# Rows 0 and 3 of the last image: separate even and odd products, other points added by VectorE, and a new order of the last two and a half images

## The chip, the core and the metric

The kernel runs on one core of a Trainium2 chip. The metric is device time in microseconds (us) of one execution; a profile of one execution gives the times of single instructions, counted from the start of its span.

## What is computed

Sixteen images of 128 channels by 64 x 64 pixels go through two layers, each with a group normalization in front and a residual sum behind it. Layer 0 is a 3 x 3 convolution of quantized inputs, done three times with three sets of weights; each of the three results is rounded to integers and clipped before they are summed. Layer 1 is an attention-like step made of 1 x 1 convolutions.

```python
def layer0(x):                      # x: 16 x 128 x 64 x 64
    v = round(clip(gn(x), -1, 1) * 127) / 127 * 0.6
    fv = patches(v) + 0.1 * patches(v) ** 3            # 3 x 3, padded by 1
    outs = [einsum(fv, g_pos[i] - g_neg[i]) for i in range(3)]
    mem = adc(outs[2])                                  # adc: scale, round, clip
    for i, bit in enumerate((2, 1, 0)):
        mem = mem + adc(outs[i]) * 2 ** bit
    return mem * output_factor + bias

def layer1(x):                      # as 64 x 128 by 128 x 4096 products
    q, k, v = Wq @ gn(x), Wk @ gn(x), Wv @ gn(x)
    num, den = exp(B) @ (exp(k) * v), exp(B) @ exp(k)
    return Wm @ (q * num / den)

y = x + layer0(x);  out = y + layer1(y)
```

## The kernel before, in words

**Convolution by points.** The 3 x 3 convolution is done with fewer products than nine. The rows of an image are cut into 16 tiles of four output rows. Each tile is turned into six sums of input rows, "points" 0 to 5 (`point`, L497). Each point is convolved along the columns, and the four output rows are sums of the points. Output rows 1 and 2 of every tile are handled together (half `h = 0`), rows 0 and 3 together (`h = 1`). Points 1 to 4 need sums that two output rows share; point 0 or point 5 belongs to one half only.

**A block** (`Block`, L562) is one image with one of the three weight sets `i`. It has two halves in PSUM, and each is a list of small operations whose names appear in the order lists, with the number `k = 2 i + h` of the half behind a dot. For one half of points 1 to 4, `u` is 0 or 1: `q1u q2u q0u q3u` are four TensorE products into `pa` and `pb` (L556); `m1u` (L579), `sdu` (L581) and `sAu` (L584) are ScalarE copies out of `pa` between them; `Bo` (L587) and `df` (L588) are VectorE sums, and `sm` is the last sum, by VectorE for an odd `k` (L594) and by an accumulating DMA from GpSimd's queue for an even `k` (L596).

The rest of a block (`rest`, L645) does the output rows. `ma` and `mc` (`middle`, L610) write two rows of small integers from the point sums. `S0` and `S3` (`total`, L615 and L618) are the sums of the other points. Then follow, for even and odd output columns in one two-bank PSUM tile: `P` (`shared`, L621), one product into one of the two banks; `bc` (`spread`, L625), VectorE, which puts that product plus the other points' sums in both banks; `o0 o1` (`outer`, L630), four products accumulated on top; `tk` (`take`, L633), ScalarE, which writes both banks as int16 into the integer tile; `bA` or `bB` (`bound`, L636), VectorE's clip; `aA` or `aB` (`add`, L641 or L643), the sum over weight sets, by VectorE or by a DMA. So the products `o0 o1` wait for `bc`, and `bc` waits for the point sums.

**The last block of the last image** (`Last`, L665) has the same work under other names: `tma tmc` are `middle`, `tS0 tS1` `total`, `tP0 tP1` `shared`, `tbc tbd` `spread`, `to0 to1` and `tp0 tp1` `outer` for rows 1 and 2 and for rows 0 and 3, `tk0 tk3` `take`, `tb0` to `tb3` `bound`, `ta0` to `ta3` the sum into `acc` by VectorE (L684). Rows 1 and 2 use the PSUM tile `py`, rows 0 and 3 use `pb`. The `h` of the code is 0 for rows 1 and 2 and 1 for rows 0 and 3.

**The end of an image** (`End`, L687): `cx0` to `cx3` scale the summed integers to float (ScalarE, L699), `cd0x` to `cd3x` add the input by accumulating DMAs (GpSimd's queue, L702), `sq0` to `sq3` square and sum (ScalarE, L364) as soon as a chunk's DMA has landed, and `ya pmy yb pvy yc yl yd` turn the sums into the normalization: VectorE and ScalarE on single columns, and two tiny products (`pmy` L383, `pvy` L392). For the last image the input is loaded early into the space of `gmat` (`Lx0` to `Lx3`, SyncE's queue, L717), added by VectorE row by row (`tx`, L724), and squared by ScalarE (`ts`); its normalization is `tna` to `tnd`.

**Layer 1** runs in four chunks ("pairs") of an image: `xn` normalizes (ScalarE, L796); `kp vp qp dn op` are products; `ek g ln ex` are ScalarE's, `ekv u oa ob oc` VectorE's; `r` (ScalarE, L782) adds the bias, `rd` (GpSimd's queue, L812) adds the input by a DMA, `st` (SyncE's queue, L813) stores. Chunks 0 and 2, and 1 and 3, share one buffer, so `xn2` waits for the store `st0` and `xn3` for `st1`. The last image has its own buffers and names with a capital (`Xn Kp Vp ...`).

**Order.** Every engine executes its instructions in the order in which the program issues them, and the program issues them by lists written out in the source. `ORDER` serves most images; `LAST` (L155) serves the end, from the middle of the last image but one. An entry such as `m10.3+1` is operation `m10.3` of turn 16 - 1 = 15, the last image's (turns count from 0); `+2` is the image before it, `+0` the tail behind it. In turn 15 the halves `.0` and `.1` of the rest, the `cx cd sq y` operations and the pairs belong to images before the last.

Of the kernel before, what the change touches and what calls it, by code (L numbers as in the profile page):

```python
# [94 lines left out]
START = "x0 xa pmx xb pvx xc xl xd gr0 er0 cp gr1 er1 pb1 pa1 cs1 cq1 cd1"  # L95

LAST = """
    cl0+2 sA1.2+2 S3.2+2 q31.2+2 lj3+2 st2+2 q10.3+2 cl1+2 P.2+2 bc.2+2 m10.3+2 q11.3+2 m11.3+2
    s0+2 q20.3+2 q21.3+2 o0.2+2 Bo.2+2 va0+2 s1+2 va1+2 sd0.3+2 o1.2+2 bA.2+2 sd1.3+2 q01.3+2
    sq1+2 sq2+2 lj2+2 gr0+2 sq3+2 q30.3+2 q00.3+2 tk.2+2 sA1.3+2 er0+2 q31.3+2 sA0.3+2 ya+2  # L100
    df.2+2 n3+2 n2+2 pmy+2 yb+2 P.3+2 bc.3+2 Bo.3+2 cp+2 q11.4+2 pvy+2 q10.4+2 yc+2 cl3+2
    df.3+2 o0.3+2 m10.4+2 m11.4+2 o1.3+2 q20.4+2 q21.4+2 yl+2 s3+2 yd+2 xn0+2 sd0.4+2 sd1.4+2
    kp0+2 vp0+2 sm.3+2 tk.3+2 P.4+2 q01.4+2 cl2+2 sm.2+2 ek0+2 va3+2 mc.4+2 s2+2 st3+2 aA.2+2
    S0.4+2 ekv0+2 bc.4+2 dn0+2 sA1.4+2 g0+2 q00.4+2 sA0.4+2 va2+2 u0+2 xn1+2 ln0+2 o1.4+2 gr1+2
    o0.4+2 q30.4+2 oa0+2 ex0+2 kp1+2 er1+2 tk.4+2 qp0+2 ob0+2 vp1+2 q11.5+2 ma.4+2 oc0+2 S3.4+2
    ek1+2 m11.5+2 pb0+2 op0+2 r0+2 ekv1+2 q31.4+2 Bo.4+2 rd0+2 q10.5+2 pa0+2 m10.5+2 st0+2
    P.5+2 q20.5+2 df.4+2 bc.5+2 sd0.5+2 q21.5+2 sd1.5+2 dn1+2 q00.5+2 g1+2 bB.3+2 xn2+1 bA.4+2
    q01.5+2 q30.5+2 o1.5+2 o0.5+2 u1+2 cs0+2 oa1+2 ln1+2 cd0+2 q31.5+2 ex1+2 tk.5+2 sA1.5+2
    sA0.5+2 cq0+2 aB.3+2 sm.4+2 kp2+1 qp1+2 vp2+1 ob1+2 ek2+1 aA.4+2 Bo.5+2 oc1+2 q10.0+1 op1+2
    m10.0+1 q20.0+1 r1+2 q11.0+1 m11.0+1 P.0+1 sd0.0+1 df.5+2 sm.5+2 ekv2+1 mc.0+1 S0.0+1  # L110
    q21.0+1 dn2+1 bB.5+2 q00.0+1 bc.0+1 o1.0+1 o0.0+1 rd1+2 g2+1 u2+1 sA0.0+1 ln2+1 aB.5+2
    sd1.0+1 ma.0+1 st1+2 q30.0+1 oa2+1 ex2+1 ob2+1 tk.0+1 xn3+1 pb1+2 S3.0+1 q01.0+1 bA.0+1
    qp2+1 oc2+1 pa1+2 kp3+1 op2+1 r2+1 vp3+1 ek3+1 cs1+2 cq1+2 ekv3+1 q31.0+1 P.1+1 bc.1+1
    q10.1+1 m10.1+1 sA1.0+1 Bo.0+1 df.0+1 rd2+1 dn3+1 o0.1+1 g3+1 u3+1 oa3+1 ln3+1 ex3+1 o1.1+1
    tk.1+1 q11.1+1 q20.1+1 cd1+2 aA.0+1 qp3+1 m11.1+1 bB.1+1 q21.1+1 sd0.1+1 q00.1+1 ob3+1
    sm.0+1 oc3+1 op3+1 sd1.1+1 aB.1+1 sA0.1+1 r3+1 q30.1+1 cx1+1 p0+1 e0+1 rd3+1 q01.1+1 cx0+1
    sA1.1+1 q31.1+1 Bo.1+1 q10.2+1 m10.2+1 df.1+1 q11.2+1 q20.2+1 cd1x+1 p5+1 y0+1 cd0x+1 P.2+1
    cx2+1 cd2x+1 m11.2+1 sd0.2+1 q21.2+1 q00.2+1 cx3+1 sd1.2+1 q01.2+1 q30.2+1 sA0.2+1 sq0+1
    sm.1+1 q10.3+1 mc.2+1 S0.2+1 q31.2+1 cd3x+1 bc.2+1 e5+1 o0.2+1 ma.2+1 sq1+1 o1.2+1 S3.2+1
    sA1.2+1 Lx0+0 m10.3+1 tk.2+1 Bo.2+1 bA.2+1 q11.3+1 m11.3+1 q20.3+1 P.3+1 df.2+1 q21.3+1  # L120
    sd0.3+1 q00.3+1 bc.3+1 Lx1+0 o1.3+1 sq2+1 sd1.3+1 q30.3+1 st3+1 sq3+1 sA0.3+1 st2+1 ya+1
    pmy+1 yb+1 q31.3+1 pvy+1 yc+1 yl+1 Bo.3+1 q01.3+1 sA1.3+1 yd+1 sm.2+1 df.3+1 sm.3+1 q10.4+1
    m10.4+1 mc.4+1 o0.3+1 xn0+1 S0.4+1 q11.4+1 tk.3+1 kp0+1 vp0+1 P.4+1 ek0+1 ekv0+1 q20.4+1
    bc.4+1 xn1+1 dn0+1 g0+1 u0+1 sd0.4+1 o0.4+1 m11.4+1 oa0+1 ln0+1 o1.4+1 ex0+1 q21.4+1 ob0+1
    tk.4+1 kp1+1 ma.4+1 qp0+1 vp1+1 aA.2+1 oc0+1 S3.4+1 ek1+1 op0+1 ekv1+1 sd1.4+1 r0+1 q00.4+1
    q01.4+1 sA1.4+1 P.5+1 rd0+1 dn1+1 g1+1 bc.5+1 q11.5+1 bA.4+1 o1.5+1 st0+1 o0.5+1 sA0.4+1
    q30.4+1 u1+1 q10.5+1 aA.4+1 ln1+1 tk.5+1 oa1+1 ex1+1 xn2+0 qp1+1 ob1+1 q31.4+1 oc1+1 bB.3+1
    Bo.4+1 op1+1 kp2+0 r1+1 m10.5+1 vp2+0 aB.3+1 q20.5+1 df.4+1 ek2+0 m11.5+1 ekv2+0 sd0.5+1
    q21.5+1 sd1.5+1 dn2+0 q30.5+1 q01.5+1 g2+0 u2+0 ln2+0 oa2+0 rd1+1 q31.5+1 sA1.5+1 st1+1
    q00.5+1 qp2+0 bB.5+1 ex2+0 aB.5+1 Bo.5+1 xn3+0 sA0.5+1 kp3+0 vp3+0 ob2+0 oc2+0 op2+0 ek3+0  # L130
    r2+0 df.5+1 tma+0 ekv3+0 sm.5+1 tS1+0 dn3+0 g3+0 u3+0 ln3+0 tP1+0 tbd+0 ex3+0 qp3+0 sm.4+1
    oa3+0 ob3+0 oc3+0 tp0+0 op3+0 tmc+0 tS0+0 tb2+0 tp1+0 Lx2+0 Lx3+0 r3+0 tP0+0 tb1+0 ta1+0
    tbc+0 to1+0 tx1+0 ta2+0 tk3+0 tx2+0 tb3+0 tsh+0 to0+0 ta3+0 tk0+0 tb0+0 ts1+0 ta0+0 ts2+0
    tx0+0 ts0+0 tx3+0 ts3+0 tna+0 tpm+0 rd2+0 tnb+0 tpv+0 tnc+0 tnl+0 tnd+0 Xn0+0 Xn2+0 Xn1+0
    Kp0+0 rd3+0 Ek0+0 Vp0+0 Xn3+0 Kp1+0 Eq0+0 Dn0+0 Vp1+0 Gg0+0 Uu0+0 Ek1+0 Eq1+0 Oa0+0 Ln0+0
    Ex0+0 Qp0+0 Kp2+0 Dn1+0 Gg1+0 Ob0+0 Oc0+0 Vp2+0 st3+0 Uu1+0 st2+0 Ek2+0 Eq2+0 Oa1+0 Ln1+0
    Ex1+0 Op0+0 Ob1+0 Qp1+0 Oc1+0 Dn2+0 Rr0+0 Op1+0 Kp3+0 Rd0+0 Gg2+0 Vp3+0 Qp2+0 Uu2+0 Rr1+0
    Rd1+0 St0+0 St1+0 Ek3+0 Oa2+0 Ln2+0 Eq3+0 Ex2+0 Dn3+0 Gg3+0 Ob2+0 Oc2+0 Uu3+0 Op2+0 Oa3+0
    Ln3+0 Ex3+0 Xa2+0 Qp3+0 Ob3+0 Xb2+0 Sa2+0 Sb2+0 Oc3+0 Op3+0 Xa3+0 Sa3+0 Xb3+0 Sb3+0
# [4 lines left out]
def conv_preact_kernel(  # L144
# [410 lines left out]
    def mm(o, w, r, start, stop):  # L555
        pe.matmul(  # L556
            o if len(r.shape) == 2 else o.rearrange("p (t w) -> p t w", w=W2), w, r,
            start=start, stop=stop, skip_group_check=True,
        )
# [398 lines left out]
```

## Time and profile before

| | |
|---|---|
| median of 3 runs | 1602.0 us (1598.37 to 1602.01) |
| profiled execution, device time | 1598.49 us |
| its span in the profile | 1596.8 us |
| TensorE busy, whole span | 1487.7 us (93%) |
| VectorE / ScalarE / GpSimd busy | 1479.8 / 1183.0 / 224.0 us |
| granted TensorE clock, mean | 0.981 |

The profile page lists busy time by engine. The trace behind it can be asked for stretches of time, for single instructions in order of time (start, duration, engine, line, operation, output and inputs, and in brackets how long the engine sat idle before and what ended that), for the DMAs issued in a stretch with their time to landing, and for the chain of work that ended last. A product of 128 x 128 weights with 512 columns shows as two TensorE records, which together take 0.86 us when products follow each other.

### The profile page before, as it was taken

Reading aid. Unit: us, or ns where it says so; the run is one execution under the profiler, and the core shown is the slowest. Engines: PE = TensorE matmul, PEld = TensorE weight load, DVE = VectorE, ACT = ScalarE, POOL = GpSimd, SP = SyncE. Lnnn points to the kernel's source line nnn. Section 1 sums busy time; section 2 is a strip of 40 time slices with the busy share of each in tenths; the row PEclk is TensorE's granted clock in tenths of the full one; section 3 lists DMA queues with packets and bytes.
Section 4 is the critical chain, followed back from the end, with each engine's and each line's share of the span. In section 5 each row is a group of like instructions: output and inputs, shape, how many; then the busy total and the mean of one; then the engine's idle time right before and its main releaser. Section 6 shows DMA issues by size and latency. Waiting matters only on the chain.

```text
span 1596.8 us, 14936 instructions
## 1 busy us (share of the span) xinstructions
PE 1487.7 (93%) x4680; PEld 563.4 (35%) x4680; DVE 1479.8 (93%) x1919; ACT 1183.0 (74%) x1857; POOL 224.0 (14%) x250
## 2 busy tenths in 40 slices
...
GB/s 186 79 92 120 103 160 171 126 204 114 148 128 164 184 119 196 120 137 141 150 205 109 156 131 150 166 132 203 117 152 132 156 176 121 196 66 119 119 158 80
DMA packets 67361, 227.03 MB, mean 142 GB/s; under 512 B 7632, under 2 KB 8272, under 8 KB 67280
## 3 DMA queue, kind: packets, MB, share of 16 engines
q0 software_dynamic: 37904, 123.42, 42.1%
...
## 4 chain that ended last, share of the span: by engine, by line
PE 58%; DMA 14%; issue 11%; DVE 11%; ACT 5%; POOL 2%; DVEq 0%; POOLq 0%; ACTq 0%; SPq 0%
PE py L556 19%; PE pa L556 18%; DMA x<-in_x_dram 5%; PE pz L749 5%; PE pb L556 5%; PE pz L759 3%; PE py L749 3%; DMA s<-s 3%; DMA acc<-y 3%; PE py L771 3%; ACT x L699 2%; DVE acc L610 1%; ACT gs L364 1%; DVE y L610 1%; DVE s L615 1%
## 5 line engine op out<-in xcount | busy, mean ns | idle before, releaser
L556 PE MATMUL py<-v,ud 128*128 128x512 f32 x760 | 357.0, 608 | 1.9 <-DVE py L625 1.3
L556 PE MATMUL pa<-cs,us 128*128 128x512 f32 x384 | 199.1, 620 | 41.7 <-DVE cs L514 31.9
L556 PE MATMUL pa<-cd,us 128*128 128x512 f32 x384 | 203.9, 622 | 11.7 <-ACT pb L581 11.7
L556 PE MATMUL pa<-cq,us 128*128 128x512 f32 x384 | 198.1, 612 | 11.3 <-ACT d L579 11.2
L556 PEld LDWEIGHTS py<-v,ud 128*128 128x128 f32 x760 | 138.9, 189 | 184.0 <-issue 148.9
L556 PE MATMUL pb<-cd,us 128*128 128x512 f32 x384 | 194.5, 602 | 1.9 <-ACT pb L581 1.7
L579 ACT ACTIVATE d<-pa 128x512 f32<-128x512 f32 x192 | 112.2, 594 | 37.8 <-PE pa L556 28.0
L812 POOL DMA_DIRECT2D xn<-x x60 | 59.9, 998 | 567.8 <-ACT xn L782 567.5
L581 ACT ACTIVATE pb<-pa 128x512 f32<-128x512 f32 x192 | 112.5, 586 | 31.3 <-PE pa L556 30.7
L584 ACT ACTIVATE s<-pa 128x512 f32<-128x512 f32 x192 | 110.4, 591 | 32.0 <-PE pa L556 29.9
L749 PE MATMUL pz<-xn,w 128*64 128x512 f32 x480 | 121.8, 607 | 1.3 <-ACT xn L796 1.2
L587 DVE SCALAR_TENSOR_TENSOR s<-d,pb 128x1024 f32<-128x1024 f32 x96 | 117.2, 1221 | 3.6 <-PE pb L556 3.2
L643 POOL DMA_DIRECT2D acc<-y x62 | 68.5, 1105 | 360.8 <-DVE y L636 212.2
L588 DVE TENSOR_TENSOR d<-s 128x1024 f32<-128x1024 f32 x96 | 117.5, 1224 | 1.6 <-ACT s L584 1.5
L633 ACT ACTIVATE y<-py 128x1024 int16<-128x1024 f32 x63 | 84.0, 1334 | 46.0 <-PE py L556 44.8
L782 ACT ACTIVATE xn<-py,scalars 128x512 f32<-128x512 f32 x120 | 76.0, 685 | 56.1 <-PE py L771 56.0
L556 PEld LDWEIGHTS pa<-cs,us 128*128 128x128 f32 x384 | 66.3, 191 | 139.6 <-issue 67.0
L556 PEld LDWEIGHTS pa<-cq,us 128*128 128x128 f32 x384 | 68.0, 190 | 119.5 <-issue 69.4
L556 PEld LDWEIGHTS pa<-cd,us 128*128 128x128 f32 x384 | 66.4, 190 | 123.6 <-ACT pb L581 56.9
L556 PEld LDWEIGHTS pb<-cd,us 128*128 128x128 f32 x384 | 70.2, 190 | 96.0 <-issue 85.2
L556 PE MATMUL py<-sv,ud 128*128 128x512 f32 x190 | 97.7, 596 | 3.3 <-ACT y L633 3.2
L596 POOL DMA_DIRECT2D s<-s x48 | 45.9, 956 | 339.5 <-DVE d L588 127.9
...
## 6 DMA issues: line engine op xcount, KB each, us to landing
xc<-in_x_dram SPq DMA_DIRECT2D x121, 512.0 KB, 5.6
acc<-y POOLq DMA_DIRECT2D x62, 512.0 KB, 5.5
x<-in_x_dram POOLq DMA_DIRECT2D x60, 512.0 KB, 10.4
xn<-x POOLq DMA_DIRECT2D x60, 512.0 KB, 4.9
out_dram<-xn SPq DMA_DIRECT2D x60, 512.0 KB, 5.1
s<-s POOLq DMA_DIRECT2D x48, 512.0 KB, 6.3
gmat<-in_x_dram SPq DMA_DIRECT2D x5, 512.0 KB, 8.9
x<-in_g_neg_dram SPq DMA_DIRECT2D x2, 576.0 KB, 11.4
```

Source lines behind the costliest of these rows:

```text
L556: pe.matmul(o if len(r.shape) == 2 else o.rearrange("p (t w) -> p t w", w=W2), w, r, start=start, stop=stop, skip_group_check=True,)
L579: f"m1{u}.{k}": lambda u=u, a=a: act.activation(d[:, u], a, AF.Copy),
L581: f"sd{u}.{k}": lambda a=a, b=b: act.activation(b, a, AF.Copy, scale=-1.0),
L584: f"sA{u}.{k}": lambda u=u, a=a: act.activation(s[:, u, 0], a, AF.Copy),
L587: f"Bo.{k}": lambda: dve.scalar_tensor_tensor(s[:, :, 1], d, 2.0, pb, ALU.mult, ALU.add),
L588: f"df.{k}": lambda: dve.tensor_tensor(d, s[:, 1], s[:, 0], ALU.subtract),
L633: act.activation(self.column(self.part(1)[0], h), y, AF.Copy)
L643: pool.dma_start(a, y, accum_op=ALU.add)
L749: pe.matmul(self.tiles(o)[h * IC : (h + 1) * IC], w, x[:, t[0] : t[1] : t[2]], start=True, stop=True)
L759: pe.matmul(o[c, t], eb[r, c], self.half(x)[r, t], start=True, stop=True, skip_group_check=True)
L782: act.activation(g[:, t], self.tiles(self.op[h]), AF.Identity, bias=bias_sb)
L812: "rd": lambda: pool.dma_start(self.r, self.x2, accum_op=ALU.add),
```

## The change

In the last block of the last image, for both halves: `shared` now makes its product once for each of the two banks, so even and odd columns start with a product of their own, and `outer` accumulates on it with nothing in between. `spread` (`tbc`, `tbd`) is gone. `take` by ScalarE is replaced by `complete`, a VectorE instruction that adds the products in PSUM and the other points' sums and writes int16. Rows 0 and 3 use the PSUM tile `pz` in place of `pb`.

The list `LAST` is written anew as a whole: 570 entries in place of 572, the same operations otherwise, in another order on all queues. Other blocks and lists are untouched.

```diff
-        def shared(self, h, y):
-            mm(y[:, 1], ud[self.i][:, h, 0], sv[:, h], True, True)
+        def shared(self, h, y, c=1):
+            mm(y[:, c], ud[self.i][:, h, 0], sv[:, h], True, True)
...
     class Last(Block):
+        def complete(self, h, y):
+            t = self.d[0] if h else ss[1][:, 1]
+            dve.tensor_tensor(self.column(self.part(1)[0], h), y, t, ALU.add)
...
-            for h, z in ((0, py), (1, pb)):
+            for h, z in ((0, py), (1, pz)):
                 o |= {
-                    f"tS{h}": lambda h=h: self.total(h), f"tP{h}": lambda h=h, z=z: self.shared(h, z),
-                    f"tb{'cd'[h]}": lambda h=h, z=z: self.spread(h, z), f"tk{3 * h}": lambda h=h, z=z: self.take(h, z),
+                    f"tS{h}": lambda h=h: self.total(h),
+                    f"tP{h}": lambda h=h, z=z: [self.shared(h, z, c) for c in range(2)],
+                    f"tk{3 * h}": lambda h=h, z=z: self.complete(h, z),
                 }
```

The parts of the order that matter below, taken from the two lists and sorted by queue (entries of other queues left out):

```diff
 ScalarE, last image but one, its second layer
-g1+2 xn2+1 ln1+2 ex1+2 tk.5+2 sA1.5+2 sA0.5+2 ek2+1
+g1+2 sd0.5+2 sd1.5+2 ln1+2 tk.5+2 xn2+1 ex1+2 sA0.5+2 sA1.5+2 ek2+1
 VectorE, the same stretch, earlier
-yd+2 sm.3+2 cl2+2 va3+2 mc.4+2 S0.4+2 ekv0+2 bc.4+2
+yd+2 ma.4+2 sm.3+2 S3.4+2 mc.4+2 va2+2 cl3+2 S0.4+2 ekv0+2 bc.4+2
 ScalarE, last image
-r3+1 cx1+1 cx0+1 sA1.1+1 m10.2+1 cx2+1 m11.2+1 sd0.2+1 cx3+1 sd1.2+1 sA0.2+1
+sA1.1+1 r3+1 sA0.1+1 cx0+1 m10.2+1 cx2+1 cx1+1 sd0.2+1 m11.2+1 cx3+1 sA0.2+1 sd1.2+1
 ScalarE, directly after
-sq0+1 sq1+1 sA1.2+1 m10.3+1 tk.2+1 m11.3+1 sd0.3+1 sq2+1 sd1.3+1 sq3+1
+sA1.2+1 sq0+1 sq1+1 sq2+1 m10.3+1 m11.3+1 tk.2+1 sd0.3+1 sd1.3+1 sq3+1
 TensorE, the same stretch
-o0.2+1 o1.2+1 q11.3+1 q20.3+1 P.3+1 q21.3+1 q00.3+1 o1.3+1 q30.3+1 pmy+1 q31.3+1
+q11.3+1 o0.2+1 o1.2+1 q20.3+1 q21.3+1 P.3+1 q00.3+1 q01.3+1 q30.3+1 pmy+1 q31.3+1
 SyncE's queue
-st1+2 Lx0+0 Lx1+0 st3+1 st2+1 st0+1 st1+1 Lx2+0 Lx3+0
+st1+2 st3+1 st2+1 Lx0+0 Lx1+0 Lx2+0 Lx3+0 st0+1 st1+1
 ScalarE, end of the last image
-ex2+0 xn3+0 sA0.5+1 ek3+0
+ex2+0 xn3+0 sA0.5+1 sA1.5+1 ek3+0
 TensorE, end of the last image
-q01.5+1 q31.5+1 q00.5+1 qp2+0 kp3+0 vp3+0 op2+0 dn3+0 tP1+0 qp3+0 tp0+0 op3+0 tp1+0 tP0+0 to1+0 to0+0
+q00.5+1 q01.5+1 q31.5+1 qp2+0 kp3+0 vp3+0 op2+0 dn3+0 qp3+0 tP1+0 tp0+0 op3+0 tp1+0 tP0+0 to1+0 to0+0
 VectorE, end of the last image
-df.5+1 tma+0 ekv3+0 sm.5+1 tS1+0 u3+0 tbd+0 oa3+0 ob3+0 oc3+0 tmc+0 tS0+0 tb2+0 tb1+0 ta1+0 tbc+0 tx1+0 ta2+0 tx2+0 tb3+0 tsh+0 ta3+0 tb0+0 ta0+0 tx0+0 tx3+0
+df.5+1 sm.5+1 ekv3+0 tma+0 tb1+0 u3+0 oa3+0 ta1+0 ob3+0 tS1+0 oc3+0 tmc+0 tb2+0 tx1+0 tsh+0 tS0+0 tk3+0 ta2+0 tb3+0 ta3+0 tx2+0 tk0+0 tb0+0 ta0+0 tx0+0 tx3+0
 ScalarE, second layer of the last image
-Xn1+0 Ek0+0 Xn3+0 Gg0+0 Ek1+0 Ln0+0 Ex0+0 Gg1+0 Ek2+0 Ln1+0 Ex1+0 Rr0+0 Gg2+0 Rr1+0
+Xn1+0 Ek0+0 Gg0+0 Ek1+0 Ln0+0 Ex0+0 Gg1+0 Ek2+0 Ln1+0 Ex1+0 Rr0+0 Xn3+0 Gg2+0 Rr1+0
```

More of the change, by code (lines that the diff above doesn't have):

```diff
@@ L97 @@
 LAST = """
[L98 to L139, printed above, removed]
+    q31.2+2 S3.2+2 cl1+2 lj3+2 sA1.2+2 P.2+2 q10.3+2 m10.3+2 lj2+2 q11.3+2 q20.3+2 bc.2+2 s1+2
@@ new lines @@
+    cl0+2 m11.3+2 Bo.2+2 o1.2+2 s0+2 sd0.3+2 va1+2 sq1+2 q21.3+2 sd1.3+2 df.2+2 sm.2+2 sq2+2
+    va0+2 o0.2+2 q30.3+2 q00.3+2 q01.3+2 sq3+2 tk.2+2 q31.3+2 P.3+2 er0+2 sA1.3+2 sA0.3+2 n3+2
+    q11.4+2 gr0+2 ya+2 pmy+2 cp+2 bc.3+2 n2+2 q10.4+2 m10.4+2 st2+2 m11.4+2 yb+2 pvy+2 o1.3+2
+    q20.4+2 q21.4+2 Bo.3+2 yc+2 yl+2 bA.2+2 df.3+2 cl2+2 o0.3+2 yd+2 sd0.4+2 xn0+2 ma.4+2
+    sm.3+2 S3.4+2 sd1.4+2 mc.4+2 kp0+2 tk.3+2 vp0+2 st3+2 q30.4+2 s2+2 q00.4+2 ek0+2 va2+2
+    cl3+2 q01.4+2 P.4+2 S0.4+2 sA0.4+2 s3+2 q10.5+2 ekv0+2 dn0+2 g0+2 bc.4+2 o0.4+2 o1.4+2
@@ new lines @@
+    m10.5+2 q20.5+2 va3+2 u0+2 ln0+2 oa0+2 ex0+2 xn1+2 kp1+2 gr1+2 tk.4+2 qp0+2 ob0+2 sA1.4+2
+    er1+2 oc0+2 vp1+2 ek1+2 pb0+2 op0+2 r0+2 rd0+2 q31.4+2 st0+2 q11.5+2 bB.3+2 P.5+2 ekv1+2
+    pa0+2 dn1+2 m11.5+2 g1+2 q21.5+2 Bo.4+2 bc.5+2 o0.5+2 aA.2+2 bA.4+2 o1.5+2 sd0.5+2 sd1.5+2
+    u1+2 oa1+2 ln1+2 cs0+2 aA.4+2 tk.5+2 cd0+2 q30.5+2 q01.5+2 q31.5+2 q00.5+2 xn2+1 bB.5+2
+    ex1+2 df.4+2 sA0.5+2 kp2+1 qp1+2 aB.3+2 ob1+2 vp2+1 sA1.5+2 q10.0+1 Bo.5+2 ek2+1 sm.4+2
+    oc1+2 op1+2 m10.0+1 aB.5+2 r1+2 df.5+2 cq0+2 q11.0+1 rd1+2 q20.0+1 P.0+1 sm.5+2 m11.0+1
@@ new lines @@
+    ekv2+1 q21.0+1 mc.0+1 sd0.0+1 q00.0+1 dn2+1 S0.0+1 bc.0+1 sd1.0+1 g2+1 oa2+1 sA0.0+1
+    q30.0+1 o1.0+1 u2+1 ln2+1 pa1+2 st1+2 ex2+1 o0.0+1 ma.0+1 pb1+2 q01.0+1 xn3+1 kp3+1 tk.0+1
+    qp2+1 ob2+1 vp3+1 cs1+2 oc2+1 op2+1 bA.0+1 q31.0+1 ek3+1 cq1+2 q10.1+1 sA1.0+1 S3.0+1
+    ekv3+1 r2+1 P.1+1 Bo.0+1 bc.1+1 dn3+1 g3+1 u3+1 q11.1+1 aA.0+1 o0.1+1 m10.1+1 oa3+1 m11.1+1
+    ln3+1 df.0+1 rd2+1 sm.0+1 cd1+2 ex3+1 o1.1+1 q20.1+1 q21.1+1 tk.1+1 bB.1+1 ob3+1 sd0.1+1
+    qp3+1 oc3+1 sd1.1+1 q01.1+1 op3+1 p5+1 e5+1 sA1.1+1 p0+1 q00.1+1 r3+1 q30.1+1 sA0.1+1
@@ new lines @@
+    q10.2+1 aB.1+1 cx0+1 m10.2+1 q31.1+1 q11.2+1 cx2+1 y0+1 rd3+1 q20.2+1 cx1+1 Bo.1+1 sd0.2+1
+    m11.2+1 cd0x+1 cd1x+1 e0+1 P.2+1 cx3+1 q00.2+1 q21.2+1 sA0.2+1 q10.3+1 sd1.2+1 q30.2+1
+    df.1+1 sm.1+1 mc.2+1 S0.2+1 q01.2+1 sA1.2+1 bc.2+1 sq0+1 ma.2+1 S3.2+1 q31.2+1 Bo.2+1
+    q11.3+1 o0.2+1 cd2x+1 sq1+1 sq2+1 o1.2+1 df.2+1 m10.3+1 q20.3+1 m11.3+1 q21.3+1 tk.2+1
+    P.3+1 sd0.3+1 q00.3+1 bc.3+1 sd1.3+1 q01.3+1 st3+1 cd3x+1 sq3+1 ya+1 q30.3+1 pmy+1 q31.3+1
+    yb+1 sA0.3+1 pvy+1 yc+1 Bo.3+1 sA1.3+1 o1.3+1 yl+1 sm.2+1 st2+1 yd+1 xn0+1 Lx0+0 df.3+1
@@ new lines @@
+    q10.4+1 m10.4+1 o0.3+1 tk.3+1 sm.3+1 mc.4+1 S0.4+1 kp0+1 vp0+1 P.4+1 ek0+1 xn1+1 q11.4+1
+    m11.4+1 ekv0+1 bc.4+1 dn0+1 g0+1 bA.2+1 u0+1 Lx1+0 o1.4+1 ln0+1 Lx2+0 ma.4+1 o0.4+1 oa0+1
+    q20.4+1 ex0+1 ob0+1 kp1+1 tk.4+1 qp0+1 vp1+1 oc0+1 bB.3+1 op0+1 ek1+1 sd0.4+1 Lx3+0 q21.4+1
+    q00.4+1 aB.3+1 r0+1 ekv1+1 bA.4+1 P.5+1 rd0+1 sd1.4+1 S3.4+1 dn1+1 g1+1 bc.5+1 q01.4+1
+    sA1.4+1 u1+1 ln1+1 st0+1 oa1+1 o0.5+1 o1.5+1 ex1+1 sA0.4+1 q30.4+1 q10.5+1 ob1+1 tk.5+1
+    qp1+1 xn2+0 q31.4+1 aA.2+1 oc1+1 m10.5+1 op1+1 kp2+0 r1+1 q11.5+1 vp2+0 q20.5+1 m11.5+1
@@ new lines @@
+    q21.5+1 bB.5+1 ek2+0 Bo.4+1 sd0.5+1 df.4+1 rd1+1 ekv2+0 st1+1 sd1.5+1 dn2+0 g2+0 q30.5+1
+    u2+0 ln2+0 ex2+0 oa2+0 ob2+0 xn3+0 q00.5+1 q01.5+1 q31.5+1 aA.4+1 qp2+0 sA0.5+1 kp3+0
+    Bo.5+1 oc2+0 sA1.5+1 df.5+1 aB.5+1 vp3+0 sm.5+1 op2+0 ek3+0 ekv3+0 tma+0 r2+0 dn3+0 g3+0
+    qp3+0 sm.4+1 tb1+0 u3+0 ln3+0 ex3+0 oa3+0 tP1+0 tp0+0 ta1+0 ob3+0 tS1+0 oc3+0 op3+0 tmc+0
+    tb2+0 tp1+0 r3+0 tx1+0 tsh+0 tS0+0 tP0+0 to1+0 tk3+0 ta2+0 tb3+0 ta3+0 to0+0 tx2+0 ts1+0
+    tk0+0 tb0+0 ta0+0 tx0+0 ts2+0 ts0+0 tx3+0 ts3+0 tna+0 tpm+0 tnb+0 tpv+0 tnc+0 tnl+0 tnd+0
```

6 lines of the change are left out of this document (added).

## The prediction

> **What bounds the kernel now.** I read the page's busy table first, then a table by stretches, then single instructions where the new list changes neighbours, then the DMAs, then the tail.
>
> ```profile
> PE 1487.7 (93%) x4680; PEld 563.4 (35%) x4680; DVE 1479.8 (93%) x1919; ACT 1183.0 (74%) x1857; POOL 224.0 (14%) x250
> ```
>
> ```profile
> 1480.00:1500.00 20.00, 19.59 (x52) 7.93 (x51) 15.66 (x26) 13.79 (x23) 0.85 (x1) 1.00 0.66 180
> 1500.00:1520.00 20.00, 20.00 (x80) 7.70 (x79) 11.28 (x15) 10.94 (x16) 1.69 (x2) 1.00 0.30 62
> 1520.00:1540.00 20.00, 17.86 (x81) 5.54 (x80) 14.48 (x18) 12.06 (x20) 3.44 (x4) 1.00 0.65 160
> 1540.00:1560.00 20.00, 11.66 (x28) 3.74 (x27) 17.55 (x26) 10.10 (x14) 1.21 (x2) 0.94 0.48 121
> ```
>
> The columns are TensorE, its weight loads, VectorE, ScalarE and GpSimd in us, the clock, the DMA share and GB/s. Up to about 1523 us TensorE is the bound; from 1540 us it is idle 8.3 of 20 us and VectorE works 17.55. So two budgets count: TensorE's idle gaps before 1523 us, and VectorE's queue behind it.
>
> TensorE's gaps (in brackets):
>
> ```profile
> 1396.50 0.38 PE L383 MATMUL pz<-y,grp 128*128 128x1 f32 x2 [1.41 <-DVE y L378]
> 1435.52 1.08 PE L749 MATMUL py<-xn,w 128*64 128x512 f32 x4 [1.30 <-ACT y L633]
> 1472.58 1.12 PE L556 MATMUL pa<-cs,us 128*128 128x512 f32 x2 [1.07 <-ACT s L584]
> 1491.54 0.38 PE L383 MATMUL pz<-y,grp 128*128 128x1 f32 x2 [0.41 <-DVE y L378]
> ```
>
> There is little to win there: the four make 4.2 us. The tail's bound is read from VectorE:
>
> ```profile
> 1541.50 1.22 DVE L625 TENSOR_TENSOR pb<-pb,d 128x1024 f32<-128x1024 f32 x1
> 1544.81 1.35 DVE L610 SCALAR_TENSOR_TENSOR y<-s,s 128x1024 int16<-128x1024 f32 x1
> 1548.92 1.23 DVE L625 TENSOR_TENSOR py<-py,s 128x1024 f32<-128x1024 f32 x1
> 1555.36 0.43 DVE L636 TENSOR_SCALAR y<-y 128x1024 int16<-128x1024 int16 x1 [1.01 <-ACT y L633]
> ```
>
> From `df.5` (1535.37) to the end of `tx3` (1559.05) VectorE has 23.68 us, in which the wait for ScalarE's `tk0` is its one gap worth a name. Last, ScalarE at the last image but one's normalization, and the DMAs issued from 1472 to 1492:
>
> ```profile
> 1483.67 0.58 ACT L579 ACTIVATE d<-pa 128x512 f32<-128x512 f32 x1
> 1484.26 1.32 ACT L633 ACTIVATE acc<-py 128x1024 int16<-128x1024 f32 x1
> ...
> 1486.47 1.14 ACT L364 ACTIVATE gs<-x,y 128x1024 int16<-128x1024 f32 x1
> ...
> 1489.33 1.15 ACT L364 ACTIVATE gs<-x,y 128x1024 int16<-128x1024 f32 x1 [1.00 <-DMA x<-in_x_dram]
> ```
>
> ```profile
> x<-in_x_dram POOLq DMA_DIRECT2D x4, 512.0 KB, 9.7
> gmat<-in_x_dram SPq DMA_DIRECT2D x2, 512.0 KB, 12.2
> out_dram<-xn SPq DMA_DIRECT2D x2, 512.0 KB, 14.4
> ```
>
> `m10.3` and `tk.2` run at 1483.67 and 1484.26, ahead of `sq2` and `sq3`. The last column is us to landing; asked one by one, `cd1x cd0x cd2x cd3x` land at 1477.9, 1480.7, 1485.4 and 1489.25.
>
> [...] `tk.2` of the image before sat behind `sq3` until 1395.45 though its products had ended. [...] 4.6 us to landing for `rd3` nearly alone, 12.6 us for `cd3x` with four transfers of SyncE's queue beside it. [...] L625 takes 1.22 us with PSUM, L588 1.22 us without, so none is lost by it.
>
> **The edit in the tail.** *Removed* from VectorE: two spreads at their pitch of 1.13 and 1.15 us, and the 1.01 us gap, since `tk0` is no longer ScalarE's: −3.29. *Added*: two completions. The nearest row is L610, 1024 columns into every second int16, 1.35 us at a pitch of 1.38; with the output of L625 it would be 1.14. I take 1.38: +2.76 (at least +2.28). *Waits*: `u3` would stand behind `g3` by 0.1 us, as `tma tb1` (1.8 us) cover nearly all of `dn3` and `g3`. *TensorE* gets two products more, 2 x 0.86 us, and `tP1` waits in `pz` for `oa3`, with `tp0 op3 tp1 tP0 to1 to0` queued behind: 12 products and `op3`, 12 x 0.86 + 1.06 = 11.4 us, while VectorE needs 12.0 us from `oa3` to `tk0` (its queue, summed by pitches). So that is hidden by 0.6 us; without that cover it would show in full. ScalarE loses two takes (2.6 us), hidden before and after. Tail: −3.29 + 2.76 + 0.1 = −0.4. `Xn3` moved behind `Rr0` (1.24 us) puts `Gg2` about 1 us and `Ek3` some 0.3 us later; `Kp3`, started at 1581.97, is still met. I take +0.1 (0 to 0.3). **Sum −0.3.**
>
> **The new order, in the sequence of time.**
> *1385 to 1397.* `sq3` still waits for its DMA (1394.3), `tk.2` stands behind it, now `P.3` does too; `P.3` starts at 1396.8 as before. 0.
> *1397 to 1436.* `tk.5` moves ahead of `xn2`, which idled 5.15 us for `st0`; so the 1.30 us gap goes. But on VectorE `ma.4` (1.38) and `S3.4` (1.22) move ahead of `ekv0` and `yb` behind `bc.3`; summing its pitches, `ekv0` ends near 1412.1 in place of 1408.9. TensorE, with three products moved ahead, is ready for `dn0` at 1411.4: 0.75 of wait. The pair's chain to `op0`, `rd0`, `st0` comes some 1.7 us later, so `kp2` waits about 1 us for `xn2`. Net +0.4 (−1.3 to +1.5).
> *1462 to 1485.* `sA1.1` gets ahead of the `cx`: the 1.07 gap goes. Now `sd0.2` and `m11.2` stand behind `cx0 cx2 cx1` (1.24 us each): `q10.2`, `q00.2` and `q10.3` wait 0.3, 1.2 and 0.7. Net +1.0 (−1.1 to +1.2).
> *1485 to 1495, the largest term.* `m10.3 m11.3 tk.2` move behind `sq0 sq1 sq2`. `sq2` needs the third input DMA, 1485.4 before. SyncE's queue now also has `Lx2 Lx3` right behind `Lx0 Lx1`, and its four start some 2 us earlier. From the page, an accumulating 512 KB takes 42.1% x 1596.8 / 123.42 MB, 2.85 us of the machine, a plain one 1.48. If the third comes no later than before, 1485.4; if all six plain ones (8.9) go ahead of it, near 1491. I take 1487. Then `sq2` 1.34 and `m10.3` 0.58: 1489.0. TensorE reached `q20.3` at 1484.92, and with +0.4 and +1.0 comes at 1486.3: **2.7 us of wait**, with all products up to `pmy` queued behind it. The old wait of 0.41 at `pmy` is absorbed: +2.3. Since 1500 to 1520 is TensorE's, this stays: 0.4 + 1.0 + 2.3 = +3.7.
> *1523 to 1535.* `kp3` waits for `xn3`, that for `st1`, that for `rd1`:
>
> ```profile
> 1525.46 4.53 DMA xn<-x
> ...
> 1530.04 3.49 DMA out_dram<-xn
> ```
>
> From the end of `op1` to `kp3` 11.05 us, 1.2 of it TensorE's wait. `q11.5` now comes behind `op1`, which starts the chain 0.86 earlier. But `sA1.5` joins `sA0.5` behind `xn3`, and `df.5` needs both: +0.55. Net −0.3.
> **Sum:** 3.7 − 0.3 − 0.3 = +3.1 on the profiled execution: 1598.5 + 3.1 = 1601.6. That execution lies 3.5 us below the median of the runs, 1602.0, the two slower of the three; on the median it gives **1605.1, I say 1605.**
>
> **Rivals.** *The chain is the bound (faster).* Spread 1.25, four outer products 3.79 and take 1.31 leave the chain that ended last: −6.4, 1595.6. For it: that chain runs through all three. Against it: VectorE's instructions in that stretch remain, and it had one gap. 0.10.
> *The DMAs land early (no change).* If the third lands by 1483.5, the wait at `q20.3` vanishes, and the gaps of 1.30 and 1.07, the 0.86 at `kp3` and 0.3 in the tail are won: −3.5, 1598.5. Against it: the share of the DMA engines stays at nine tenths or more from 1476 to 1492. 0.15.
> *The squares stand behind SyncE's transfers (slower).* One mechanism, at `m10.3`: the third DMA lands at 1491, so the wait is 6.7 in place of 2.7: +7.1, 1609.1. It decides from a landing at 1488.7 on, where the sum passes +4.8. For it: stores before took 14.4 us and ended after `cd3x`, so the queues do share. 0.25.
> My forecast has 0.50; its own range is that of a landing from 1485.4 to 1488.7, 1603 to 1607. That the edit does not do what it says I leave out: the list names both completions.
>
> **Numbers.** Slower or faster means by over 0.3%, 4.8 us, about what a measurement of this kernel can tell from no change. Slower 0.25; within 0.65 (0.50 and 0.15); faster 0.10. The range 1598 to 1610 takes in all but the faster rival and a late tail of the slower one, under 0.2.
>
> **What would show it.** Right: in ScalarE's queue three squares (L364) ahead of the copy L579, a TensorE gap of 2 to 4 us released by L579 some 10 us ahead of L383; no gap released by L633 near 1435; VectorE without a gap between the completions, each near 1.36 us; from `df.5` to the last L724 about 23.3 us. Wrong: no gap at `q20.3`, completions above 1.6 us, `tk0` waiting for TensorE over 1 us, or new TensorE gaps above 1 us between 1500 and 1523.

## The result and the profile after

In six runs of each, the changed kernel has a median of 1609.61 us and the kernel before 1602.01 us: **ratio 1.0053, interval 1.0035 to 1.007, slower** by more than the 0.3% that the forecast named as its measure. The forecast was 1605, in a range of 1598 to 1610, with "no change" as the likeliest case.

The profiled execution took 1610.77 us with a span of 1609.1, against 1596.8 before. From here on code lines of `kernel.py` are one higher than before up to L665 and seven higher behind the new method `complete` (L671). Everything in this execution lies 1.17 us later already at `pvx` (L393), a tiny product of an image's first normalization, ahead of the first changed entry: 1375.53 in place of 1374.36. So I subtract 1.17 when I set positions of the two traces side by side, and +11.1 us of difference is left to explain. That is more than the 7.6 us between the medians, since the profiled execution before lies 3.5 us below its median and the one after 1.2 us above. The traces tell where time goes; what a cause costs is read from the timed ratios.

The page's busy line, and then the table by stretches:

```profile
PE 1492.7 (93%) x4684; PEld 565.2 (35%) x4684; DVE 1480.1 (92%) x1919; ACT 1181.5 (73%) x1855; POOL 224.1 (14%) x250
```

```profile
1480.00:1500.00 20.00, 15.65 (x36) 6.56 (x35) 9.71 (x19) 10.27 (x18) 0.85 (x1) 0.91 0.86 229
...
1520.00:1540.00 20.00, 20.00 (x74) 6.88 (x66) 10.05 (x14) 11.38 (x17) 3.86 (x4) 1.00 0.56 118
1540.00:1560.00 20.00, 12.96 (x51) 4.09 (x48) 13.07 (x16) 6.95 (x11) 0.00 (x0) 0.91 0.26 62
```

The work is nearly the same: of the 5.0 us that TensorE has more, 1.7 are the two added products, and the rest are products that ran slowly (below). In the first row TensorE is idle for 4.35 us, 0.41 before; in the last VectorE, which worked 17.55 of the 20 us, works 13.07. The clock, the third number from the end, is 0.91 in both, where before it was 1.00 and 0.94. TensorE's own instructions name the two places:

```profile
1490.59 3.30 PE L557 MATMUL pa<-cq,us 128*128 128x512 f32 x4 [4.35 <-ACT d L580]
...
1545.49 3.50 PE L756 MATMUL pz<-xn,w 128*64 128x512 f32 x8 [5.05 <-ACT xn L803]
```

The first is `q20.3` with `q21.3`, the second `kp3` with `vp3`. In the kernel before, `q20.3` alone (`q21.3` came later) and `kp3` with `vp3` look so:

```profile
1484.92 1.02 PE L556 MATMUL pa<-cq,us 128*128 128x512 f32 x2
...
1534.91 1.94 PE L749 MATMUL pz<-xn,w 128*64 128x512 f32 x8 [1.21 <-ACT xn L796]
```

Each line of after holds two facts: the wait in brackets, and a duration that is too long. Four records like those of the first line took 1.98 us where TensorE had not been idle, and the eight of the second took 1.94 before. Stretches of 2 us from `kp3` on show a slow clock with it; the clock column is down to half and back at 1.00 only from 1550 on:

```profile
1546.00:1548.00 2.00, 2.00 (x8) 0.49 (x4) 1.52 (x2) 0.41 (x1) 0.00 (x0) 0.50 0.00 0
...
1550.00:1552.00 2.00, 1.14 (x18) 0.51 (x16) 1.74 (x2) 1.27 (x2) 0.00 (x0) 1.00 0.00 0
```

**The first wait** is read from ScalarE's queue: the squares (L365), the copies `m10.3 m11.3` (L580), `tk.2` (L634):

```profile
1484.94 1.15 ACT L365 ACTIVATE gs<-x,y 128x1024 int16<-128x1024 f32 x1 [2.27 <-DMA x<-in_x_dram]
...
1488.81 1.15 ACT L365 ACTIVATE gs<-x,y 128x1024 int16<-128x1024 f32 x1 [2.63 <-DMA x<-in_x_dram]
...
1489.96 1.06 ACT L580 ACTIVATE d<-pa 128x512 f32<-128x512 f32 x2
```

These are the second and third of three squares ahead of the copy; each begins when its input DMA lands, the third's, issued at 1476.24, after 12.48 us. `m10.3`, whose product had ended by 1479.2, begins behind the third square at 1489.96. That is the mechanism of the forecast.

**The second wait** is read from the chain of what ended last, and from the DMAs issued from 1525 to 1550 (last column: us to landing):

```profile
1531.40 4.70 DMA xn<-x
...
1536.15 7.97 DMA out_dram<-xn
```

```profile
acc<-y POOLq DMA_DIRECT2D x2, 512.0 KB, 8.4
...
s<-s POOLq DMA_DIRECT2D x1, 512.0 KB, 12.2
out_dram<-xn SPq DMA_DIRECT2D x1, 512.0 KB, 8.0
```

`rd1` takes 4.70 us (4.53 before), but the store `st1` behind it 7.97 where it took 3.49. GpSimd's queue of after, then that of before, shows what runs beside it:

```profile
1531.40 0.84 POOL L819 DMA_DIRECT2D xn<-x  x1 [12.35 <-ACT xn L789]
1531.93 2.39 POOL L644 DMA_DIRECT2D acc<-y  x2
1533.19 2.07 POOL L597 DMA_DIRECT2D s<-s  x1
```

```profile
1515.58 0.84 POOL L643 DMA_DIRECT2D acc<-y  x1 [2.47 <-DVE y L636]
1525.46 0.85 POOL L812 DMA_DIRECT2D xn<-x  x1 [9.04 <-ACT xn L782]
1532.03 1.19 POOL L643 DMA_DIRECT2D acc<-y  x1 [5.72 <-DVE y L636]
```

Before, `aA.4` went out 9.9 us ahead of `rd1`, and `aB.5`, with `sm.4` next, 6.6 us behind it, since its clip `bB.5` came late on VectorE. In the new list `aA.4` stands behind `rd1` and `bB.5` comes early, so `aA.4 aB.5 sm.4`, three accumulating DMAs, leave in one go right behind `rd1`, and `st1` is under way together with them: the DMA share in its 7.97 us stands at 1.06 to 1.08, against 0.83 in the 3.49 us before. The front part did not show these entries, and the prediction did not cost them.

**The tail** is as forecast in kind: the spreads and ScalarE's `tk0` and `tk3` are gone, and two completions stand in their place:

```profile
1561.49 1.29 DVE L671 TENSOR_TENSOR y<-pz,d 128x1024 int16<-128x1024 f32 x1
...
1566.31 1.29 DVE L671 TENSOR_TENSOR y<-py,s 128x1024 int16<-128x1024 f32 x1 [0.69 <-PE py L557]
```

### The profile page after: what moved, and what is told of

Its sections match the earlier page's. It is cut to its first block, busy times and chain, and to the rows that moved or that the text cites. A ratio compares the mean times of both kernels' runs of the same rounds, so it can differ in the third digit from the quotient of the medians.

```text
span 1609.1 us, 14938 instructions
## 1 busy us (share of the span) xinstructions
PE 1492.7 (93%) x4684; PEld 565.2 (35%) x4684; DVE 1480.1 (92%) x1919; ACT 1181.5 (73%) x1855; POOL 224.1 (14%) x250
## 4 chain that ended last, share of the span: by engine, by line
PE 58%; DMA 14%; DVE 13%; issue 9%; ACT 5%; POOL 1%; DVEq 0%; ACTq 0%; POOLq 0%; SPq 0%
PE py L557 19%; PE pa L557 18%; PE pz L756 6%; PE pb L557 5%; DMA x<-in_x_dram 5%; DMA s<-s 3%; PE pz L766 3%; PE py L756 3%; PE py L778 3%; DMA acc<-y 2%; ACT x L706 2%; DMA xc<-in_x_dram 2%; DVE acc L611 1%; DVE py L626 1%; DVE y L611 1%
## 5 line engine op out<-in xcount | busy, mean ns | idle before, releaser
L557 PE MATMUL pa<-cd,us 128*128 128x512 f32 x384 | 203.5, 620 | 11.5 <-ACT pb L582 11.4
L580 ACT ACTIVATE d<-pa 128x512 f32<-128x512 f32 x192 | 112.2, 594 | 34.8 <-PE pa L557 22.6
L634 ACT ACTIVATE y<-py 128x1024 int16<-128x1024 f32 x62 | 82.5, 1330 | 41.4 <-PE py L557 40.3
## 6 DMA issues: line engine op xcount, KB each, us to landing
gmat<-in_x_dram SPq DMA_DIRECT2D x5, 512.0 KB, 15.1
```

Of the source, the lines that this page charges most:

```text
L557: pe.matmul(o if len(r.shape) == 2 else o.rearrange("p (t w) -> p t w", w=W2), w, r, start=start, stop=stop, skip_group_check=True,)
L580: f"m1{u}.{k}": lambda u=u, a=a: act.activation(d[:, u], a, AF.Copy),
L634: act.activation(self.column(self.part(1)[0], h), y, AF.Copy)
```

## The experiments

Theory: the edit is worth nothing, and two independent waits of the new order cost the time: W1, the copy behind the squares at `q20.3`; W2, the store `st1` beside three accumulating DMAs; each is made longer by a slow TensorE clock behind it. Rivals: the edit or the tail itself is slower; there is only one cause; the clock is not a cost of its own. Each kernel was timed in five rounds against the kernel before; ratios are to that kernel, and a diff shows entries of one queue of `LAST`.

### Undoing W1

```diff
 after; ScalarE
-sq0+1 sq1+1 sq2+1 m10.3+1 m11.3+1 tk.2+1 sd0.3+1 sd1.3+1 sq3+1
+sq0+1 sq1+1 m10.3+1 m11.3+1 tk.2+1 sd0.3+1 sd1.3+1 sq2+1 sq3+1
```

> The changed kernel (1609.6 us), with the third square of the last image but one (sq2) put back behind the two copies, the take-over and the next two copies on ScalarE, directly ahead of sq3; nothing else moves. Theory, that the wait of 4.35 us for the copy behind the squares is a cause: that gap shrinks below 1 us and the slow products after it (3.30 us for two, in place of 1.98) are gone; but pmy still needs the fourth square and so the fourth input DMA (landed at 1492.6), so that of the 5.7 us some 2.8 show: 1606.5 us. Rival, that the edit (completion on VectorE, tile pz) costs the time: within 1 us of 1609.6. Second rival, that only the DMA's landing counts and ScalarE's order is indifferent: the gap moves whole to pmy, within 1 us of 1609.6.

Measured: 1607.78 us, ratio 1.0043 (1.0028 to 1.0057). `q20.3` and `pmy` in its trace:

```profile
1484.09 1.98 PE L557 MATMUL pa<-cq,us 128*128 128x512 f32 x4 [0.63 <-ACT d L580]
...
1492.29 0.38 PE L384 MATMUL pz<-y,grp 128*128 128x1 f32 x2 [2.78 <-DVE y L379]
```

The wait at `q20.3` falls from 4.35 to 0.63, but 2.78 us come up at `pmy`, which needs all four squares and so all four input DMAs. Most of the wait has only moved. W2 is untouched: 5.06 us at `kp3`.

### Undoing W2

```diff
 after; GpSimd
-aA.2+1 rd1+1 aA.4+1 aB.5+1 sm.4+1
+aA.2+1 aA.4+1 rd1+1 aB.5+1 sm.4+1
 after; VectorE
-bB.5+1 Bo.4+1 df.4+1 ekv2+0 u2+0 oa2+0 ob2+0
+Bo.4+1 df.4+1 ekv2+0 u2+0 oa2+0 bB.5+1 ob2+0
```

> The changed kernel with two moves round the DMA chain of the last image but one's second chunk: the accumulating DMA aA.4 issued ahead of the residual DMA rd1 (its clip is long done), and the clip bB.5 done later, after oa2 as in the kernel before, so that aB.5 and sm.4 are issued after rd1 has landed. Theory, that three accumulating DMAs issued in one go with rd1 slow the store st1 (8.0 us in place of 3.5): the store takes 3.5 to 4.5 us, TensorE's wait for xn3 falls from 5.05 to below 1 us and the slow products after it (3.50 us for four, in place of 1.94) are gone: 1609.6 - 4.3 - 1.5 - about 1 in the tail = 1603 us. Rival, that the edit costs the time: within 1 us of 1609.6. Second rival, that the store is slow by itself at this place: the wait stays above 3 us, 1608 us or more.

Measured: 1603.49 us, ratio **1.0013** (1.0003 to 1.0023). The stores take 2.7 us, and the trace has no gap at `kp3`:

```profile
out_dram<-xn SPq DMA_DIRECT2D x2, 512.0 KB, 2.7
```

Two entries moved take back 0.0040 of 0.0053, some 6.4 us: W2 is the larger cause. W1 is still there, 4.50 us.

### Undoing both

Both diffs above together.

> Both of these moves in one kernel. Theory of two independent waits: the gains add, 1609.6 - 3 - 6.6 = 1600 us, at or below the kernel before (1602.0). Rival, that the second wait takes the place of the first (one slack shared by both): no faster than the better of the two alone, 1603 us.

Measured: 1603.27 us, ratio 1.0017 (1.0007 to 1.0027), not to be told from the run with W2 alone undone: the gains do not add. At `q20.3` 0.47 us are left, and 3.12 us come up at `pmy`, as in the first experiment:

```profile
1496.25 0.38 PE L384 MATMUL pz<-y,grp 128*128 128x1 f32 x2 [3.12 <-DVE y L379]
```

So putting the square back mostly moves W1 down the queue. From `pvx` to the end the two traces are 1.5 us apart, less than these intervals can tell.

### Loads behind the store

```diff
 the kernel with both undone; SyncE
-st1+2 st3+1 st2+1 Lx0+0 Lx1+0 Lx2+0 Lx3+0 st0+1 st1+1
+st1+2 st3+1 st2+1 st0+1 Lx0+0 Lx1+0 Lx2+0 Lx3+0 st1+1
```

> Both moves of e3_both, and the four loads of the last image's input (Lx0 to Lx3) behind the store st0 on SyncE's queue, some 45 us later. Theory, that the input DMAs cd0x to cd3x are slow because SyncE's loads share the DMA engines with them: their times to landing fall (the fourth from 14.8 to about 10 us), TensorE's wait of 3.1 us at pmy, which took the place of the one at the copies, falls below 1 us, and the time is some 3 us below e3_both: ratio to the kernel before 0.998 to 1.000. Rival, that these DMAs are slow by themselves (four accumulating transfers one after the other): times to landing within 1 us of those of e3_both, no gain, ratio 1.0015 or more. Second rival: the loads now slow rd1 and st1, and the wait for xn3 comes back.

Measured: 1599.81 us, ratio **0.9994** (0.9983 to 1.0005). `pmy` in its trace:

```profile
1492.55 0.38 PE L384 MATMUL pz<-y,grp 128*128 128x1 f32 x2 [0.70 <-DVE y L379]
```

The wait at `pmy` falls from 3.12 to 0.70, and `kp3` waits 1.40 (1.21 in the kernel before). The third input DMA lands after 10.8 us and the fourth after 11.7, in place of 12.6 and 15.1. So what was left of W1 came from the four loads that SyncE's queue sent ahead of the input's accumulating DMAs. By its ratio the kernel is level with the one before, with the edit and nearly all of the new order in place. Its one trace is less clear: from `pvx` to the end it has 224.5 us, against 222.4 before, so up to 2 us of loss may be left there. The loads moved with the squares still ahead of the copy were not run.

### Causing each in the kernel before

```diff
 before; ScalarE (first kernel)
-sq0+1 sq1+1 sA1.2+1 m10.3+1 tk.2+1 m11.3+1 sd0.3+1 sq2+1
+sq0+1 sq1+1 sA1.2+1 sq2+1 m10.3+1 tk.2+1 m11.3+1 sd0.3+1
 before; GpSimd (second kernel)
-rd0+1 aA.4+1 aB.3+1 rd1+1 aB.5+1 sm.4+1
+rd0+1 aB.3+1 rd1+1 aA.4+1 aB.5+1 sm.4+1
 before; VectorE (second kernel): bB.5+1 from behind oa2+0 to behind oc1+1
```

> The kernel before, with one entry moved: the third square (sq2) stands ahead of the copy m10.3 on ScalarE, so the copy and the product q20.3 behind it wait for the third input DMA; loads, stores and the tail keep their order. Theory (the wait comes from the squares' place): TensorE waits 2 to 3 us at q20.3, released by the copy, because that DMA landed at 1485.4 and TensorE arrives at 1484.9; the gap of 0.41 at pmy goes; [...] Ratio 1.0015 (1.0005 to 1.0025). Rival (only the loads queued ahead make the DMA late enough to matter): wait under 1 us, ratio at most 1.000.

Measured: 1600.77 us, ratio 1.0014 (1.0004 to 1.0025). `q20.3` in its trace:

```profile
1486.69 1.13 PE L557 MATMUL pa<-cq,us 128*128 128x512 f32 x2 [1.35 <-ACT d L580]
```

With the loads as in the kernel before, the wait is 1.35 us, below the 2 to 3 expected. Another 0.67 is waited at the product ahead of it, which had no gap before; it needs `sA1.2`, which stands behind two squares in both kernels, so that part is not the moved square's. The products behind the wait run at their usual 1.13. The time is the expected one. So W1 has two parts: the square ahead of the copy costs about 0.0014 by itself, and in the new list the loads make the input DMAs later on top (12.6 us for the third, 10.8 with the loads behind the store).

> The kernel before, without the edit, with only the DMA order of the changed kernel at its second-last chunk: the clip bB.5 done early, and the accumulating DMAs aA.4 and aB.5 issued directly behind rd1, with sm.4 behind them. Theory, that this alone makes the store st1 slow: the store takes 7 to 8 us in place of 3.5, TensorE's wait for xn3 rises from 1.2 to about 5.5 us, with slow products after it, and the time is 5 to 7 us above the kernel before: ratio 1.003 to 1.0045. Rival, that it needs the rest of the new order too: within 1 us of the kernel before, ratio below 1.001.

Measured: 1606.15 us, ratio **1.0045** (1.0029 to 1.006), without a line of the edit. `kp3`, and then the store among the DMAs issued from 1520 to 1545 (in this kernel all code lines here are one higher than before):

```profile
1539.18 3.68 PE L750 MATMUL pz<-xn,w 128*64 128x512 f32 x8 [6.26 <-ACT xn L797]
```

```profile
out_dram<-xn SPq DMA_DIRECT2D x1, 512.0 KB, 8.4
```

The store takes 8.4 us, the wait is 6.26 and the products behind it take 3.68; in the changed kernel these were 8.0, 5.05 and 3.50. W2 is shown from both sides.

### The edit alone

```diff
 before; the changed functions, and on TensorE's queue
-dn3+0 tP1+0 qp3+0 tp0+0
+dn3+0 qp3+0 tP1+0 tp0+0
 VectorE: tbc+0 and tbd+0 out, all else as before
```

In the first of two kernels the program issues `tP1` ahead of `oa3`, `tP1` writes `pz` before `oa3` has read it, and the last pair is computed from other numbers; only its time is used. In the second it is issued behind `oa3` and waits for it.

> The edit of the last block alone (two products of their own, completion on VectorE, tile pz), in the order list of the kernel before: its two spreads are taken out of the list and the product tP1 stands behind qp3, since pz comes free later; everything else in the old order. Theory, that the new order and not the edit costs the time: by the working of the prediction for the tail -0.4 us, so 1601.6 us, ratio to the kernel before 0.999 to 1.001. Rival, that the edit costs the time: 1606 us or more.

Measured: 1600.2 us, ratio 0.9994 (0.9981 to 1.0007).

> The edit of the last block alone once more, in the order list of the kernel before, with tP1 now behind oa3, so that the numerator of the fourth chunk is read before its PSUM tile is used again (the run before it in this place computed that chunk from other numbers, and is of use for its time only). Theory, that the order and not the edit costs the time: ratio to the kernel before 0.998 to 1.001, some 0.2 to 0.5 us less in the tail. Rival, that the edit costs the time: 1.003 or more.

Measured: 1599.47 us, ratio 1.0003 (0.9989 to 1.0017). The edit is worth nothing that can be measured, with or without that wait. The tail rival falls.

### Keeping TensorE busy while it waits

Into the changed kernel, four products that nobody reads ahead of `q20.3` and five ahead of `kp3`:

```diff
+"fa": lambda: [mm(pz[:, 0], us[0][:, 0, 1], cs[:, 0], True, True) for _ in range(4)],
+"fb": lambda: [mm(pz[:, 0], us[0][:, 0, 1], cs[:, 0], True, True) for _ in range(5)],
```

> The changed kernel with products that nobody reads in TensorE's two long waits: four (3.4 us) ahead of q20.3 and five (4.3 us) ahead of kp3, into the free tile pz; everything else the same, the waits for the copy and for the store remain. Theory, that the slow products after the waits come from TensorE's clock[...]: the two products after the first wait take 1.98 us in place of 3.30, the four after the second 1.94 in place of 3.50, and the time is 3 to 4 us below the changed kernel: 1606 us. Rival, that they are slow for a reason of their own (semaphores, the DMA traffic): no change, 1609 to 1610 us.

Measured: 1605.89 us, ratio 1.0038 (1.0025 to 1.0052). The two products, and then the stretch of the second, in this kernel's trace:

```profile
1490.01 1.98 PE L557 MATMUL pa<-cq,us 128*128 128x512 f32 x4 [1.38 <-ACT d L580]
...
1543.23 1.94 PE L758 MATMUL pz<-xn,w 128*64 128x512 f32 x8 [0.57 <-ACT xn L805]
```

```profile
1540.00:1560.00 20.00, 17.22 (x62) 6.29 (x61) 15.30 (x20) 8.53 (x13) 1.72 (x2) 1.00 0.22 46
```

The products behind the waits are back at 1.98 and 1.94, and the clock of the stretch is 1.00, though the copy and the store are still waited for. 3.30 − 1.98 and 3.50 − 1.94 make 2.9 us of cost that is neither a wait nor work. The ratio falls by 0.0015, 2.4 us, but the two intervals overlap, and in this trace the third input DMA landed 1.7 us later, counted from `pvx`, than in the changed kernel. The slow products go with the slow clock, 3.30 and 3.50 at 0.50 against 1.98 and 1.94 at 1.00; what that costs in all is an estimate.

### The gains of the new order by themselves

```diff
 before with the edit (first kernel), without it (second); ScalarE
-g1+2 xn2+1 ln1+2 ex1+2 tk.5+2
+g1+2 ln1+2 ex1+2 xn2+1 tk.5+2
-cx0+1 sA1.1+1
+sA1.1+1 cx0+1
 TensorE: q11.5+1 from behind dn1+1 to behind kp2+0
 VectorE: u1+2 from behind bA.4+2 to ahead of it
```

> The edit on the list before (spreads out, tP1 behind oa3), with the three moves of the new list that remove a TensorE gap and none of its others: the pair's u1 ln1 ex1 ahead of xn2 and tk.5 right behind it, sA1.1 ahead of cx0, q11.5 behind kp2. Theory (the gains of the new list are real and were hidden by the two waits): the gaps of 1.30 at qp1 and 1.07 at q11.2 go, the one before kp3 shrinks by 0.9; 3.0 us, ratio 0.998 (0.997 to 0.9995). Rival (a gap that is closed comes back at the next wait): ratio 0.9995 to 1.001, with a new gap of about 1 us at xn2, kp2 or behind the cx.

Measured: 1598.11 us, ratio 0.999 (0.9982 to 0.9999).

> The same three moves on the kernel before, without the edit. Theory (the edit itself is worth 0.3 us): ratio within 0.001 of that of the same moves with the edit, 0.998. Rival (the edit's shorter tail counts): 0.001 or more slower than with the edit.

Measured: 1597.73 us, ratio 0.9987 (0.9978 to 0.9995). So the edit makes no difference here either. Both gain about half of what was expected, because one wait came back in another place, here in the kernel with the edit:

```profile
1485.47 1.13 PE L557 MATMUL pa<-cs,us 128*128 128x512 f32 x2 [1.73 <-ACT s L585]
```

That product waits for `sA1.2`, which stands behind two squares; TensorE is earlier, the input DMAs are not (the first square begins 107.4 us after `pvx`, 106.4 in the kernel before). The last kernel therefore also has:

```diff
 before with the edit and the moves above; ScalarE
-sq0+1 sq1+1 sA1.2+1 m10.3+1 tk.2+1 m11.3+1 sd0.3+1 sq2+1
+sA1.2+1 m10.3+1 sq0+1 tk.2+1 m11.3+1 sd0.3+1 sq1+1 sq2+1
 SyncE
-st1+2 Lx0+0 Lx1+0 st3+1 st2+1 st0+1 st1+1 Lx2+0 Lx3+0
+st1+2 st3+1 st2+1 st0+1 Lx0+0 Lx1+0 st1+1 Lx2+0 Lx3+0
```

> The edit with the three gap moves, and in addition what its own trace shows to have come in their place: there TensorE waited 1.73 us for the copy sA1.2, which stood behind two squares that wait for the first input DMA. Here sA1.2 and m10.3 stand ahead of the first square and sq1 behind sd0.3, and Lx0 Lx1 go behind st0 on SyncE's queue. Theory (the gap moves win 3 us once nothing waits for the input DMAs): no TensorE gap above 0.5 us before the pmy product, at pmy at most 0.8, no gap above 0.5 at kp3; ratio 0.998 (0.9970 to 0.9988). Rival (the input DMAs set the pace of this stretch whatever the order, so the wait moves to pmy): a gap of 1.5 us or more at pmy, ratio 0.999 as without these moves.

Measured: 1599.39 us, with the kernel before at 1603.07: ratio **0.9982** (0.9971 to 0.9994), faster than both kernels, though less than 0.3% faster than the one before. `pmy` in its trace:

```profile
1492.42 0.38 PE L384 MATMUL pz<-y,grp 128*128 128x1 f32 x2 [0.45 <-DVE y L379]
```

The waits are as small as expected but for one of 0.66 at `P.3`, and `kp3` has none. How much of the ratio these moves earn stays open: its interval overlaps that of the kernel with the first three moves alone, and in the one profiled execution the stretch from `pvx` to the end is 222.2 us, against 222.4 before and 221.6 with the three moves. In it 0.74 us came back at `kp2`, which waits for `xn2`.

## Why the prediction was wrong

In the trace, positions less 1.17 us, the +11.1 us arise so:

| stretch | forecast | trace |
|---|---|---|
| up to TensorE's arrival at `q20.3` | +1.4 | +0.15 |
| `q20.3` to `kp0` | +2.3 | +4.6 |
| `kp0` to `kp3` | −0.3 | +4.6 |
| `kp3` to the last image's normalization | −0.3 | +1.7 |
| sum | +3.1 | +11.1 |

**"1523 to 1535: net −0.3" is the step that failed.** It followed the chain `rd1`, `st1`, `xn3`, `kp3` and took both transfers' times, 4.53 and 3.49 us, over unchanged from the row before. It moved instructions of ScalarE and TensorE only, and did not ask which DMAs of GpSimd's queue the new list puts beside the store. With 8.0 for 3.5 the chain is 4.5 longer, and the trace has +4.6. The number to do it with stood in the prediction itself: 2.85 us of all DMA engines for an accumulating 512 KB. By that estimate three of them are 8.6, beside a store that was priced with the neighbours it had before. The experiment that sets the three behind `rd1` in the kernel before costs 0.0045, 7.2 us; that which moves them away gains 0.0040.

**"1485 to 1495, the largest term"** was right in mechanism: three squares ahead of the copy, a gap released by L580, the landing estimated at 1487 and measured at 1487.6 (1488.7 less 1.17). That closeness is in part luck, as 1487 was picked between 1485.4 and 1491 with no working. The size of the wait was wrong for two reasons. The term ahead of it, "1462 to 1485: net +1.0" (its own terms, 2.2 less 1.07, make 1.1), did not come. None of the waits of 0.3, 1.2 and 0.7 shows in the trace; the one gap there is 0.45, at `P.2`, ended by VectorE. So TensorE came at 1485.1, not 1486.3, and the wait was 4.35 in place of 2.7. The lateness that didn't come saved no time, since the next wait ended at the landing; it lengthened that wait. And the four records behind the wait took 1.3 us too long.

**The clock had no term at all.** The forecast counted a wait by its length alone. In the trace the clock is 0.50 from 1546 to 1548, and the products took 3.50 for 1.94 behind 5.05 us of idleness; one kernel fell to 0.50 behind 2.63 us (last section). The profile before had the slow clock too, behind the tail's 7.42 us wait (0.50 from 1560 to 1568), in a row that the prediction did not use:

```profile
1560.00:1580.00 20.00, 15.01 (x84) 5.18 (x88) 8.73 (x23) 11.66 (x19) 0.00 (x0) 0.72 0.00 0
```

Neither the forecast wait of 2.7 us nor the slower rival's 6.7 us had a term for it.

**"Sum −0.3" for the tail was about right, in part by luck.** From `df.5` to the end of the last L731 the forecast was 23.3 us. In the changed kernel it is 24.9, since `kp3`'s slow products make VectorE wait 1.33 us at L808; where `kp3` does not wait (W2 undone) it is 23.45, against 23.68 before. Two errors offset each other there. The next instruction follows a completion after 1.19 and 1.33 us, not 1.38. And the cover of 0.6 us did not hold: `tk0` waits 0.69 us for TensorE (0.66 with W2 undone), under the 1 us named as a bound. The prediction set TensorE's 11.4 us against VectorE's 12.0 as if both began together; `tP1` starts 0.74 us after `oa3` does, and the products took 12.0. "1385 to 1397: 0" and "1397 to 1436: +0.4" came out near (−0.1 and +0.1, read at `P.3` and `op1`, with 1.41 us of wait at `xn2` where about 1 was forecast).

**The rivals.** The slower case gave 1609.1, close to the measured 1609.6, but by luck: it put 4.0 us on top of the forecast for a landing at 1491, and the landing was 1487.6. Over half of the loss came from a store that no case mentioned.
